# Grouping the attention products of a graph layer and moving its residual additions within the block

## The chip, the cores and the metric

The kernel runs on one core of a Trainium2 chip. The metric is the time of one execution on the device in microseconds; lower is better. A core has a matrix engine (TensorE, PE in the profile, with its weight loads as PEld), a vector engine (VectorE, DVE), an activation engine (ScalarE, ACT), a general engine (GpSimd, POOL) and an engine that here issues nearly all transfers (SyncE, SP). Each runs its own queue of instructions in the order of the program and waits on semaphores for the others.

## The reference

The input `x` holds 128 graphs of 64 nodes with 768 features, `adj` their 64 x 64 adjacency matrices. The features are normalised and rectified, go through two layers of the same kind, and the result is added to `x`:

```
h = max(layernorm(x), 0)
for l in 0, 1:
    u = triangular mix of (h W_left h^T) and (h W_right h^T) / sqrt(768)
    e = exp(u) * adj
    attention = e / (sum(e, axis=2) + 1e-10)
    h_lin = h W_lin + b_lin
    ctx = attention @ h_lin
    h = max((ctx - mean) / (std + 0.001) * ln_a + ln_b, 0)
out = x + h
```

All of it is float32. What matters here is the end of the second layer: `ctx`, its normalisation, the rectifier and the addition of `x` (the residual).

## The kernel before, in words

The 128 graphs are cut into NB = 16 blocks of 8 graphs, 512 nodes each. Each layer has two passes over the blocks. `pass_one` makes the attention matrices and leaves them in DRAM. `pass_two`, which the change touches, makes `h_lin` with a fast scheme of 15 block products in place of 18, multiplies by the attention, and normalises. `last` is true in layer two.

In `pass_two`, `linear(u, ...)` runs the 15 products of block `u` in the order of the list `ORDER`. Products share four accumulators named X, Z, Y and V in `ORDER`; the profile shows the tiles' own names, through `NAME`: X is tile Z there, Z is V, Y is X, V is Y. Accumulator X serves products 0, 2, 4, 6, 8 and 10, Y serves 3, 7 and 11, V serves 5, 9, 12 and 14, Z serves 1 and 13. A product adds to what its accumulator holds, and `read` (L300 for ScalarE, the helper at L245 for VectorE) moves the running sum into `hl` after each; the next product of the same accumulator has to wait for that read. The matrix products have line L1006. `fresh` (L995) starts an accumulator, by a ScalarE copy of the bias where one is wanted. The mean of `h_lin` is taken out of the weights beforehand, so that only the standard deviation is left to work out.

The order is written by hand (`manual_schedule`): each block has 30 slots, two a product, one run in the middle of the product and one after its reads, and `put(n, f)` hangs a piece of work on slot n; a slot of 30 or more is carried to the next block. All engines' instructions are issued in that one order, so a slot says behind what a piece of work stands on its engine's queue, not when it runs. SP issues a transfer when it comes to it and all that it must wait for is done, and may be far ahead of the others.

At the head of block u, ahead of slot 0, `load_h` (L368) asks for the tokens of block u+1: two tiles `ht` of 768 KB. ScalarE scales and rectifies them at slots 9 to 14 (`affine`, L379, two activations a slot, one on each of the two tiles), and POOL makes sums of them from slot 15 on (L245). `load_at` (L1036) brings the attention at slot 4.

The attention products of block u-1 and what follows them run inside block u. Two functions can do this. `finish(u, r)` makes half a block: `context` multiplies 16 small products into both buffers of the PSUM tile `aux` (L1048), ScalarE squares and sums them (L1193) and takes the root (L1195), VectorE inverts it (L1198, L1199). In layer two VectorE then scales by that and by `ln_a` (L1203), POOL adds `ln_b` (L1206), and `done` lets VectorE rectify and add the residual tile `xr` (L1217); two stores a tile go out from SP (L1219). `residual` (L1133) loads the two `xr` tiles of half a block with four transfers. `finish_block(u, more)` makes the whole block with one group of products (L1071), which writes to `aux` and to accumulators X and Y; VectorE copies the two parts that lie there away (L1143), the squares follow at slots 25 to 29 (L1154), the deviation and its inverse at 30 and 32 (L1158 to L1163), the scaling at 33 to 36 (L1168). A block has four row tiles, named (r, k) by half and place.

Before the change layer one uses `finish_block` for blocks 0 to 12 and `finish` for the last ones. Layer two uses `finish` throughout: the first half after product 0 of the next block with its steps at slots 6, 7, 8, 11, 12, the second half after product 7 with its steps at 20, 21, 22, 30, 30. The loads of the next residual half hang on the second `done` of each half. The last block of layer two has a form of its own (`last_block`, `finish_last`).

Of the kernel before, what the change touches and what calls it, by code (L numbers as in the profile page):

```python
# [10 lines left out]
F32 = mybir.dt.float32  # L11
I32 = mybir.dt.int32
AF = mybir.ActivationFunctionType
ALU = mybir.AluOpType
# [3 lines left out]
def kernel(  # L18
# [12 lines left out]
    nc = tc.nc  # L31
    B, S, H = x.shape
    L = w_lin.shape[0]
    P = 128
# [4 lines left out]
    PAIR = P // S  # L39
# [3 lines left out]
    NB = B * S // T  # L43
# [12 lines left out]
    NBB = T // S  # L56
# [10 lines left out]
    def put(slot, *fs):  # L67
        plan.setdefault(slot, []).extend(fs)
# [880 lines left out]
    rows = {}  # L949
# [62 lines left out]
    def pass_two(l, aside):  # L1012
        last = l == L - 1
        with tc.tile_pool(name=f"two{l}", bufs=2, reuse_waits="tile") as sp, \
# [59 lines left out]
            def batch(r, k, h):  # L1074
                return 4 * (h if k == 0 else 1 - h) + r + 2 * k

            XS = {}
# [27 lines left out]
            def finish_last(u, r):  # L1105


                cx = context(u, r)
                zs = [sp.tile([P, H], F32, name="z", bufs=4) for _ in range(2)]
                squares = sp.tile([P, Q, H], F32, name="hl", bufs=2)  # L1110
                two = "p (n d) -> p n d"
                xs = XS[u, r]
                of = stat.tile([P, 2, 2], F32, name="of", bufs=1)
                ss, rs = ([of[:, n, k:k + 1] for k in range(2)] for n in range(2))
                for k in (1, 0):
                    nc.scalar.activation(squares[:, k].rearrange(two, n=2), cx[k], AF.Square, accum_out=ss[k])
                    nc.vector.tensor_tensor(zs[1 - k].rearrange(two, n=2), cx[1 - k],  # L1117
                                            rows["a"].rearrange(two, n=2), op=ALU.mult)
                    nc.scalar.activation(rs[k], ss[k], AF.Sqrt, bias=floor, scale=1.0 / (H - 1.0))
                for k in (1, 0):  # L1120
                    nc.vector.tensor_scalar_add(rs[k], rs[k], EPS_LN)  # L1121
                    nc.vector.reciprocal(rs[k], rs[k])  # L1122
                    nc.vector.scalar_tensor_tensor(zs[k], zs[k], rs[k], rows["-b"], op0=ALU.mult, op1=ALU.max)  # L1123
                    nc.vector.tensor_add(xs[k], xs[k], zs[k])  # L1124
                    for h, queue in enumerate((nc.sync, nc.scalar)):
                        queue.dma_start(out[u * NBB + batch(r, k, h)], xs[k][h * S:(h + 1) * S])
                return []

            def residual(u, r):
                XS[u, r] = [sp.tile([P, H], F32, name="xr", bufs=4) for _ in range(2)]  # L1130
                for k in range(2):
                    for h in range(PAIR):
                        nc.sync.dma_start(XS[u, r][k][h * S:(h + 1) * S], x[u * NBB + batch(r, k, h)])  # L1133

            def finish_block(u, more):

                parts = context_block(u)
                tiles = ((0, 0), (0, 1), (1, 0), (1, 1))
                zs = {t: sp.tile([P, H], F32, name="z", bufs=4) for t in tiles}
                cut = (slice(0, T), slice(T, H))  # L1140

                for t in ((1, 1), (1, 0)):
                    nc.vector.tensor_copy(zs[t][:, cut[0]], parts[t][0])  # L1143
                    parts[t][0] = zs[t][:, cut[0]]
                    if t == (1, 1):
                        AHEAD.append(fresh(l, 0, more))
                ss = stat.tile([P, Q, 2], F32, name="ssb", bufs=2)
                sd = stat.tile([P, Q], F32, name="sdb", bufs=2)
                rs = stat.tile([P, Q], F32, name="rsb", bufs=2)

                def squares(t):
                    junk = zs[0, t[1]]
                    for n in range(2):
                        nc.scalar.activation(junk[:, cut[n]], parts[t][n], AF.Square,  # L1154
                                             accum_out=ss[:, 2 * t[0] + t[1], n:n + 1])

                def deviation():
                    nc.vector.reduce_sum(sd, ss, axis=mybir.AxisListType.X)  # L1158
                    nc.scalar.activation(sd, sd, AF.Sqrt, bias=floor, scale=1.0 / (H - 1.0))

                def inverse():
                    nc.vector.tensor_scalar_add(rs, sd, EPS_LN)
                    nc.vector.reciprocal(rs, rs)  # L1163

                def scaled(t):
                    by = rs[:, 2 * t[0] + t[1]:2 * t[0] + t[1] + 1]
                    for n in range(2):
                        nc.scalar.activation(zs[t][:, cut[n]], parts[t][n], AF.Copy, scale=by)  # L1168
                    kept(u, *t, zs[t])

                order = ((1, 1), (1, 0), (0, 0), (0, 1))
                for f, slots in ((squares, (25, 26, 28, 29)), (scaled, (33, 34, 35, 36))):
                    for n, t in zip(slots, order):
                        put(n, lambda f=f, t=t: f(t))
                put(30, deviation)
                put(32, inverse)

            def kept(u, r, k, z):
                for h in range(PAIR):
                    nc.sync.dma_start(ROWS[u][batch(r, k, h)], z[h * S:(h + 1) * S])  # L1180

            def finish(u, r):

                cx = context(u, r)
                zs = [sp.tile([P, H], F32, name="z", bufs=4) for _ in range(2)]
                if last and not u and not r:
                    residual(u, r)
                two = "p (n d) -> p n d"
                ss = stat.tile([P, 2], F32, name="ss", bufs=2)
                sd = stat.tile([P, 2], F32, name="sd1", bufs=2)  # L1190
                rs = stat.tile([P, 2], F32, name="rs1", bufs=2)
                for k in range(2):
                    nc.scalar.activation(zs[k].rearrange(two, n=2), cx[k], AF.Square, accum_out=ss[:, k:k + 1])  # L1193

                nc.scalar.activation(sd, ss, AF.Sqrt, bias=floor, scale=1.0 / (H - 1.0))  # L1195

                def inverse():
                    nc.vector.tensor_scalar_add(rs, sd, EPS_LN)  # L1198
                    nc.vector.reciprocal(rs, rs)  # L1199

                def scaled(k):
                    if last:
                        nc.vector.scalar_tensor_tensor(  # L1203
                            zs[k].rearrange(two, n=2), cx[k], rs[:, k:k + 1],
                            rows["a"].rearrange(two, n=2), op0=ALU.mult, op1=ALU.mult)
                        nc.gpsimd.tensor_add(zs[k], zs[k], rows["b"])  # L1206
                        return
                    if (u, r, k) == (NB - 1, 1, 1):
                        nc.vector.tensor_scalar_mul(zs[k].rearrange(two, n=2), cx[k], rs[:, k:k + 1])
                    else:  # L1210
                        nc.scalar.activation(zs[k].rearrange(two, n=2), cx[k], AF.Copy, scale=rs[:, k:k + 1])
                    kept(u, r, k, zs[k])

                def done(k):
                    if last:
                        xs = XS[u, r]
                        nc.vector.scalar_tensor_tensor(xs[k], zs[k], 0.0, xs[k], op0=ALU.max, op1=ALU.add)  # L1217
                        for h in range(PAIR):
                            nc.sync.dma_start(out[u * NBB + batch(r, k, h)], xs[k][h * S:(h + 1) * S])  # L1219
                        if k and u + r < NB - 1 and (u, r) != (NB - 2, 0):  # L1220
                            residual(u + r, 1 - r)

                steps = [lambda f=f, k=k: f(k) for f in (scaled, done) for k in range(2)]
                return [inverse] + (steps if last else steps[:2])

# [35 lines left out]
            for u in range(NB):  # L1261
                turn = not last and u >= NB - 2
                put(4, lambda u=u: load_at(u))
                if u + 1 < NB:
# [11 lines left out]
                        aside[u]()  # L1276
                    ends = {}
                    if u and last:
                        ends = {0: ((u - 1, 0), (6, 7, 8, 11, 12)), 7: ((u - 1, 1), (20, 21, 22, 30, 30))}
                    elif u > NB - 3:  # L1280
                        ends = {5: ((u - 1, 0), (16, 17, 18)), 11: ((u - 1, 1), (28, 29, 30))}
                    elif u:
                        ends = {12: (u - 1, None)}
# [3 lines left out]
                else:  # L1287
# [8 lines left out]
                                {4: ((u, 0), (50, 51, 52))})  # L1296
                    else:
                        last_block(u)
                        put(8, lambda: residual(u - 1, 1))
                        ends = ({0: ((u - 1, 0), (12, 13, 15, 19, 31)), 9: ((u - 1, 1), (28, 29, 30, 39, 41))},  # L1300
                                {2: ((u, 0), (44, 48, 51, 61, 62))})
                    linear(u, (0,), 0, ends[0], (1,))
# [62 lines left out]
```

## Time and profile before

| what | value |
|---|---|
| median of 3 runs | 2648.96 us |
| lowest, highest | 2647.83, 2654.08 us |
| the profiled execution's own time | 2648.42 us |
| its span from the first to the last instruction | 2646.6 us |
| mean granted TensorE clock | 0.995 |

Layer two's second pass takes roughly the last sixth of the span, from about 2190 us on. A time in the views below counts from the span's start. A row of the timeline gives start and length in us, engine, line, operation, and the tile written, an arrow, and the tiles read; several like instructions in a row are merged into one with a count. A row of the waits names who waited, an arrow, for whom, then the total in us, how often, and the longest. A row of the groups by line gives the durations in ns as min/median/max.

### The profile page before, as it was taken

Reading aid. Unit: us, or ns where it says so; the run is one execution under the profiler, and the core shown is the slowest. Engines: PE = TensorE matmul, PEld = TensorE weight load, DVE = VectorE, ACT = ScalarE, POOL = GpSimd, SP = SyncE. Lnnn points to the kernel's source line nnn. Section 1 sums busy time; section 2 is a strip of 40 time slices with the busy share of each in tenths; the row PEclk is TensorE's granted clock in tenths of the full one; section 3 lists DMA queues with packets and bytes.
Section 4 is the critical chain, followed back from the end, with each engine's and each line's share of the span. In section 5 each row is a group of like instructions: output and inputs, shape, how many; then the busy total and the mean of one; then the engine's idle time right before and its main releaser. Section 6 shows DMA issues by size and latency. Waiting matters only on the chain. (4 is left out here: it accounts for less than half of the span.)

```text
span 2646.6 us, 47202 instructions
## 1 busy us (share of the span) xinstructions
PE 2591.6 (98%) x18122; PEld 2217.1 (84%) x18122; DVE 1780.6 (67%) x2888; ACT 935.4 (35%) x1969; POOL 1763.1 (67%) x1392
## 2 busy tenths in 40 slices
PE   9899999999999999999999999999999989999998
PEld 8788888888888888888798888888888878887886
DVE  7878787777768445554456667677666676666667
ACT  5522223223113244454542222122222335555453
POOL 4766676666668657676276666667666657878786
PEclk9999999999999999999999999999999999999999
DMA  7443534343421354445794424253532215555655
GB/s 220 113 111 86 124 93 110 93 119 79 98 60 56 123 156 149 159 139 182 219 282 101 121 68 108 71 129 93 136 98 70 67 49 157 157 167 166 177 161 146
DMA packets 258465, 331.84 MB, mean 125 GB/s; under 512 B 56002, under 2 KB 190402, under 8 KB 258242
## 3 DMA queue, kind: packets, MB, share of 16 engines
q1 hardware_dynamic: 241442, 320.56, 44.3%
q10 hardware_dynamic: 16800, 8.26, 1.2%
q8 instruction: 145, 2.38, 0.4%
q14 instruction: 78, 0.64, 0.1%
HBM read 213.39 MB, written 115.34 MB: 124 GB/s over the span
## 5 line engine op out<-in xcount | busy, mean ns | idle before, releaser
L245 POOL TENSOR_TENSOR g<-ht 128x512 f32<-128x512 f32 (+1 forms) x620 | 785.9, 1279 | 420.8 <-PE Z L702 71.6
L245 POOL TENSOR_TENSOR g<-g,g 128x512 f32<-128x512 f32 (+1 forms) x310 | 397.9, 1291 | 136.7 <-PE C L702 22.0
L245 POOL TENSOR_TENSOR g<-ht,g 128x512 f32<-128x512 f32 (+1 forms) x272 | 346.1, 1282 | 164.8 <-PE Z L702 42.8
L702 PE MATMUL X<-g,g 128*128 128x256 f32 (+1 forms) x1080 | 252.9, 377 | 6.0 <-DVE m L914 6.0
L1006 PE MATMUL Z<-g,g 128*128 128x256 f32 x1024 | 244.1, 380 | 3.5 <-ACT hl L300 3.2
L702 PE MATMUL C<-g,g 128*128 128x256 f32 x1008 | 239.7, 381 | 4.9 <-POOL g L245 2.2
L702 PEld LDWEIGHTS X<-g,g 128*128 128x128 f32 x1080 | 203.0, 191 | 34.8 <-DVE m L914 6.8
L702 PE MATMUL Y<-g,g 128*128 128x256 f32 (+1 forms) x968 | 225.7, 376 | 3.8 <-POOL g L245 3.8
L1006 PEld LDWEIGHTS Z<-g,g 128*128 128x128 f32 x1024 | 191.6, 190 | 35.8 <-issue 4.1
L379 ACT ACTIVATE ht<-ht,b_col,a_col 128x256 f32<-128x256 f32 x384 | 196.1, 591 | 69.0 <-DMA ht<-h 53.8
L702 PEld LDWEIGHTS C<-g,g 128*128 128x128 f32 x1008 | 190.5, 190 | 32.9 <-POOL g L245 3.5
L702 PE MATMUL Z<-g,g 128*128 128x256 f32 (+1 forms) x936 | 217.0, 375 | 0.0
L702 PE MATMUL D<-g,g 128*128 128x256 f32 x880 | 209.8, 381 | 1.8 <-POOL g L245 1.8
L702 PEld LDWEIGHTS Y<-g,g 128*128 128x128 f32 x968 | 182.0, 190 | 27.8 <-POOL g L245 4.2
L702 PE MATMUL V<-g,g 128*128 128x256 f32 (+1 forms) x840 | 194.6, 375 | 3.1 <-POOL g L245 1.6
L702 PEld LDWEIGHTS Z<-g,g 128*128 128x128 f32 x936 | 174.5, 190 | 23.1
L702 PEld LDWEIGHTS D<-g,g 128*128 128x128 f32 x880 | 168.1, 191 | 25.7 <-POOL g L245 2.5
L1006 PE MATMUL X<-g,g 128*128 128x256 f32 x768 | 182.7, 379 | 0.0
L702 PEld LDWEIGHTS V<-g,g 128*128 128x128 f32 x840 | 157.6, 191 | 23.3 <-POOL g L245 1.7
L1206 POOL TENSOR_TENSOR z<-z,b 128x768 f32<-128x768 f32 x62 | 112.7, 1829 | 81.7 <-DVE z L1203 77.2
L245 DVE TENSOR_TENSOR m<-m,Y 128x512 f32<-128x512 f32 (+2 forms) x196 | 126.5, 667 | 58.4 <-ACT m L910 35.7
L245 DVE TENSOR_TENSOR m<-m,D 128x512 f32<-128x512 f32 x180 | 118.2, 677 | 70.0 <-ACT m L910 51.3
(222 smaller groups left out, 4612.0 us busy)
## 6 DMA issues: line engine op xcount, KB each, us to landing
ht<-h SPq DMA_DIRECT2D x126, 768.0 KB, 6.3
h<-xb SPq DMA_DIRECT2D x124, 384.0 KB, 6.6
z<-z SPq DMA_DIRECT2D x128, 192.0 KB, 3.1
x<-z SPq DMA_DIRECT2D x128, 192.0 KB, 5.4
xr<-in_x_dram SPq DMA_DIRECT2D x120, 192.0 KB, 3.8
out_dram<-xr SPq DMA_DIRECT2D x120, 192.0 KB, 2.7
x<-in_x_dram SPq DMA_DIRECT2D x112, 192.0 KB, 5.4
g<-form SPq DMA_DIRECT2D x40, 256.0 KB, 5.6
```

The lines of the kernel that those rows point to most:

```text
L245: (eng.tensor_add if sign == "+" else eng.tensor_sub)(o, a, b)
L379: nc.scalar.activation(ht, ht, AF.Relu, bias=cols[1][:, c:c + 1], scale=cols[0][:, c:c + 1])
L702: nc.tensor.matmul(o, w[:, c, g * P:(g + 1) * P], t, start=(new and g == c == at == 0), stop=(c == K2 - 1), skip_group_check=True)
L1006: nc.tensor.matmul(p[:, n], b[t][:, c, r * P:(r + 1) * P], w[s][:, c, :], start=(i in FIRST and i not in PRELOAD and n == c == 0), stop=(c ...
L1206: nc.gpsimd.tensor_add(zs[k], zs[k], rows["b"])
```

## The change

In layer two the attention products of blocks 0 to 12 are made by `finish_block`, as in layer one, called after product 12 of the next block. Blocks 13 and 14 keep `finish`, block 13 with its two halves after products 5 and 10 of block 14. In `finish_block` the scaling goes to VectorE with `ln_a`, in two parts a tile, POOL adds `ln_b`, and the new `done` adds the residual: tiles (0,0) and (0,1) at slots 39 and 42, which are slots 9 and 12 of the block after, tiles (1,0) and (1,1) at 58 and 61, which are slot 28 of that block and slot 1 of the one behind it. The residual loads no longer hang on `done`; they have slots of their own, 20 and 29 (13 and 29 in block 14, 3 and 9 in block 15). The tiles `z` get six buffers in place of four, the tiles `xr` five in place of four.

```diff
             def residual(u, r):
-                XS[u, r] = [sp.tile([P, H], F32, name="xr", bufs=4) for _ in range(2)]
+                XS[u, r] = [sp.tile([P, H], F32, name="xr", bufs=5) for _ in range(2)]
...
             def finish_block(u, more):
-                zs = {t: sp.tile([P, H], F32, name="z", bufs=4) for t in tiles}
+                zs = {t: sp.tile([P, H], F32, name="z", bufs=6 if last else 4) for t in tiles}
...
+                def done(t):
+                    z, xs = zs[t], XS[u, t[0]][t[1]]
+                    nc.vector.scalar_tensor_tensor(xs, z, 0.0, xs, op0=ALU.max, op1=ALU.add)
+                    for h in range(PAIR):
+                        nc.sync.dma_start(out[u * NBB + batch(*t, h)], xs[h * S:(h + 1) * S])
+
                 def scaled(t):
                     by = rs[:, 2 * t[0] + t[1]:2 * t[0] + t[1] + 1]
                     for n in range(2):
-                        nc.scalar.activation(zs[t][:, cut[n]], parts[t][n], AF.Copy, scale=by)
-                    kept(u, *t, zs[t])
+                        if last:
+                            nc.vector.scalar_tensor_tensor(zs[t][:, cut[n]], parts[t][n], by, rows["a"][:, cut[n]],
+                                                           op0=ALU.mult, op1=ALU.mult)
+                        else:
+                            nc.scalar.activation(zs[t][:, cut[n]], parts[t][n], AF.Copy, scale=by)
+                    if last:
+                        nc.gpsimd.tensor_add(zs[t], zs[t], rows["b"])
+                    else:
+                        kept(u, *t, zs[t])
 
                 order = ((1, 1), (1, 0), (0, 0), (0, 1))
-                for f, slots in ((squares, (25, 26, 28, 29)), (scaled, (33, 34, 35, 36))):
+                if last:
+                    order = ((0, 0), (0, 1), (1, 0), (1, 1))
+                for f, slots in ((squares, (25, 26, 28, 29)), (scaled, (33, 34, 35, 36))) + (
+                        ((done, (39, 42, 58, 61)),) if last else ()):
...
             def finish(u, r):
-                if last and not u and not r:
-                    residual(u, r)
...
-                        if k and u + r < NB - 1 and (u, r) != (NB - 2, 0):
-                            residual(u + r, 1 - r)
...
                     if u and last:
-                        ends = {0: ((u - 1, 0), (6, 7, 8, 11, 12)), 7: ((u - 1, 1), (20, 21, 22, 30, 30))}
+                        for r in range(2):
+                            put(29 if r else 20 if u < NB - 2 else 13, lambda u=u, r=r: residual(u - 1, r))
+                    if u > NB - 3 and last:
+                        ends = {5: ((u - 1, 0), (16, 17, 18, 21, 22)), 10: ((u - 1, 1), (25, 26, 27, 36, 38))}
                     elif u > NB - 3:
                         ends = {5: ((u - 1, 0), (16, 17, 18)), 11: ((u - 1, 1), (28, 29, 30))}
...
                         last_block(u)
-                        put(8, lambda: residual(u - 1, 1))
+                        put(3, lambda: residual(u - 1, 0))
+                        put(9, lambda: residual(u - 1, 1))
```

The tiles `z` of `finish` and `finish_last` get six buffers too.

More of the change, by code (lines that the diff above doesn't have):

```diff
@@ L1108, in finish_last @@
                 cx = context(u, r)
-                zs = [sp.tile([P, H], F32, name="z", bufs=4) for _ in range(2)]
+                zs = [sp.tile([P, H], F32, name="z", bufs=6) for _ in range(2)]
                 squares = sp.tile([P, Q, H], F32, name="hl", bufs=2)
@@ L1184, in finish @@
                 cx = context(u, r)
-                zs = [sp.tile([P, H], F32, name="z", bufs=4) for _ in range(2)]
-                if last and not u and not r:
-                    residual(u, r)
+                zs = [sp.tile([P, H], F32, name="z", bufs=6 if last else 4) for _ in range(2)]
                 two = "p (n d) -> p n d"
```

## The prediction

> **What bounds the kernel now.** I read the page's busy table first, then who waits for whom in the stretch that the change touches (layer two's second pass, 2190 to 2600 us), then the cost of one block there beside a block of layer one's second pass, which already has the form that the change brings.
>
> ```profile
> span 2646.6 us, 47202 instructions
> ...
> PE 2591.6 (98%) x18122; PEld 2217.1 (84%) x18122; DVE 1780.6 (67%) x2888; ACT 935.4 (35%) x1969; POOL 1763.1 (67%) x1392
> ```
>
> ```profile
> engine line waited for: us in total, times, longest us
> ACT hl L300 <- PE Z L1006: 141.4, 41, 6.7
> ...
> POOL g L245 <- ACT ht L379: 6.6, 14, 0.5
> ```
>
> In this stretch every engine waits for TensorE or for one another; no row has PE itself waiting. So the stretch ends with TensorE, and the change can win only what it takes from TensorE's queue, and loses whatever makes TensorE wait. The price of a block is the distance between equal places in neighbouring blocks (windows: length, then busy time of PE, PEld, DVE, ACT, POOL):
>
> ```profile
> 1088.95:1117.79 28.84, 28.84 (x157) 23.76 (x159) 15.76 (x23) 13.34 (x35) 20.63 (x17) 1.00 0.29 88
> 2370.35:2399.55 29.20, 29.20 (x153) 23.59 (x153) 19.93 (x25) 15.08 (x32) 23.20 (x16) 1.00 0.57 167
> ```
>
> The first row is layer one (one group of attention products a block, L1071), the second layer two (two groups, L1048). TensorE is busy through both at full clock. The difference is 0.36 us.
>
> **The change, part by part.**
>
> *Products.* Blocks 1 to 13 of layer two go from two groups to one: 13 x 0.36 = **4.7 us less**. Block 14 keeps two, block 15 its own form. Nothing else leaves TensorE's queue.
>
> *Copies, squares, scaling.* One group adds two VectorE copies a block (0.69 and 0.68 us, as the layer-one rows below have them) and cuts four scalings into eight. VectorE has 19.93 of 29.20 us busy, so some 3 us more fit; the copies, the preload behind them and the squares stand where layer one has them, under TensorE at full cover. I cost this at nothing; without cover it is the third rival.
>
> *The residual additions and loads.* Here the order on SP's queue changes, and SP issues strictly in program order. These are its rows for one block now:
>
> ```profile
> 2371.02 3.05 SPq L1219 DMA_DIRECT2D out_dram<-xr  x4
> 2374.12 2.52 SPq L1133 DMA_DIRECT2D xr<-in_x_dram  x4
> 2376.74 1.00 SPq L1036 DMA_DIRECT2D at<-att  x2
> 2383.50 3.05 SPq L1219 DMA_DIRECT2D out_dram<-xr  x4
> 2386.59 2.52 SPq L1133 DMA_DIRECT2D xr<-in_x_dram  x4
> 2389.28 0.95 SPq L368 DMA_DIRECT2D ht<-h  x2
> ```
>
> The last row is the load of the token halves `ht` for the block after the next boundary. It stands at the head of the next block's code, but SP reaches it 10.3 us before that block's first context group (2399.55), since the last thing ahead of it is the addition at slot 12. After the change the last things ahead of it are the addition of tile (1,0) at slot 28 with two stores, and four residual loads at slot 29. SP stands still at the store until VectorE has added. That wait has the rest of SP's queue behind it: first the four residual loads, then the two `ht` loads.
>
> When does it come now? The block's last products and VectorE's reads of them, in layer one, where the order of the last three products is that of the new kernel:
>
> ```profile
> 1091.62 1.99 PE L1006 MATMUL V<-g,g 128*128 128x256 f32 x8
> 1093.45 1.89 PE L1006 MATMUL Y<-g,g 128*128 128x256 f32 x8
> 1095.18 1.03 PE L1006 MATMUL Z<-g,g 128*128 128x256 f32 x4
> ```
>
> ```profile
> 1090.04 0.69 DVE L1143 COPY z<-Z 128x512 f32<-128x512 f32 x1 [0.36 <-PE Z L1071]
> 1090.65 0.68 DVE L1143 COPY z<-X 128x512 f32<-128x512 f32 x1
> ...
> 1093.66 0.69 DVE L245 TENSOR_TENSOR hl<-hl,V 128x512 f32<-128x512 f32 x1 [1.73 <-PE V L1006]
> ```
>
> Let S be the start of the next block's first product, 1095.18. VectorE reads product 13 from S-1.52; the addition at slot 28 is next in its queue and begins 0.61 later, at S-0.91. Its length (min, median, max in ns), then the row of landing times of the 108 stores of L1219, then that of the 28 loads of the tile `ht`, both in this stretch:
>
> ```profile
> L1217 DVE SCALAR_TENSOR_TENSOR xr<-z,xr x60: 951/2023/2432, 2206.2 to 2626.0; 128x768 f32<-128x768 f32 x60
> ```
>
> ```profile
> DMA to landing us min/median/max: 2.6/2.7/4.1
> ```
>
> ```profile
> DMA to landing us min/median/max: 4.4/6.6/8.1
> ```
>
> With the median 2.02 us the addition ends at S+1.11. SP issues the two stores at S+1.14 and S+1.74 (0.6 each), the second lands 2.7 later at S+4.45. The first residual tile's two loads go out meanwhile. With five `xr` buffers the second tile takes the buffer of the very tile just stored (four tiles a block: tile (1,1) of one block is five after tile (1,0) of the block before), so SP waits until S+4.5; two issues of 0.64, and the `ht` loads go out at S+5.9 and S+6.53. The landing row gives 4.4 to 8.1 us. I take 6.4, a little under the median, because two loads instead of four stand right before. The second half then lands at **S+12.9**.
>
> When is it needed? Now ScalarE and TensorE in the middle of a block:
>
> ```profile
> 2378.82 1.89 PE L1006 MATMUL Y<-g,ht 128*128 128x256 f32 x8
> 2380.54 1.89 PE L1006 MATMUL Z<-g,g 128*128 128x256 f32 x8
> 2382.27 1.89 PE L1006 MATMUL X<-g,g 128*128 128x256 f32 x8
> 2384.09 1.52 PE L1048 MATMUL aux<-hl,at 64*64 64x384 f32 x16
> 2385.54 1.99 PE L1006 MATMUL Z<-g,ht 128*128 128x256 f32 x8
> ```
>
> ```profile
> 2379.02 0.60 ACT L300 ACTIVATE hl<-Z 128x512 f32<-128x512 f32 x1 [2.37 <-PE Z L1006]
> 2379.51 4.03 ACT L379 ACTIVATE ht<-ht,b_col,a_col 128x256 f32<-128x256 f32 x8
> 2383.44 0.58 ACT L300 ACTIVATE hl<-Z 128x512 f32<-128x512 f32 x1
> ```
>
> The PE rows are products 5, 6, 7, a context group, 8. ScalarE reads product 4, puts eight `ht` activations through (first and second half in turn), then reads product 6, out of the bank on which product 8 accumulates. That read ends at 2384.02, 5.20 us after product 5 began. Product 8 has until then 1.5 us in hand, which is the context group; the change moves that group to the block's end, and three products of 1.73 are 5.19: **no slack is left**. Any delay of the activations becomes a wait of TensorE before product 8. The second activation (first of the second half) begins 1.18 after product 5's start, that is at S + 5 x 1.73 + 1.18 = S+9.83. The half lands at S+12.9: **3.1 us of wait a block**.
>
> It first happens in block 3 (the first store at slot 28 is in block 2) and last in block 14, which still loads block 15: 12 blocks, 12 x 3.1 = 37.2 us. Bounds: with the shortest addition (0.95) and the quickest load (4.4) nothing is left (below nothing isn't possible, since TensorE's products stay); with 2.43 and 8.1 it is 5.2 us, 62 us in all.
>
> *The clock.* TensorE's granted clock after its two longest waits behind VectorE (2.9 and 3.1 us):
>
> ```profile
> PE X L702 <- DVE m L914: 6.0, 2, 3.1
> ```
>
> ```profile
> 834.00:838.00 4.00, 1.10 (x6) 0.70 (x5) 3.96 (x5) 0.83 (x2) 3.70 (x3) 1.00 0.00 0
> ...
> 2134.00:2136.00 2.00, 0.12 (x1) 0.00 (x0) 1.97 (x2) 0.42 (x1) 2.00 (x2) 1.00 0.00 0
> 2136.00:2138.00 2.00, 0.78 (x2) 0.69 (x3) 2.00 (x4) 0.42 (x1) 1.70 (x2) 0.66 0.00 0
> 2138.00:2140.00 2.00, 2.00 (x7) 1.55 (x6) 2.00 (x4) 0.00 (x0) 0.36 (x1) 0.50 0.00 0
> 2140.00:2142.00 2.00, 2.00 (x11) 1.77 (x10) 2.00 (x5) 0.00 (x0) 2.00 (x2) 0.98 0.00 0
> ```
>
> After the first the clock (third number from the right) stays at 1.00; after the second it is half for about 3.4 us (0.34 x 2 / 0.5 + 2 + 0.08), which costs 1.7 us of products. One of two: I estimate half of the twelve waits, 6 x 1.7 = 10 us; bounds 0 and 20.
>
> The Trainium skill ("TensorE: Matmul & The Clock Gate", Part 1) has the clock fall to half only after a whole idle window of about 3.4 us. By that rule a wait of 3.1 us would cost no clock and the sum would come out about 10 us lower; the 2136 row, a fall after 3.1 us, speaks against it here.
>
> *Sum*, against the profiled execution's 2648.42 us (span 2646.6 and 1.8 around it; the median shown is 2648.96, 0.5 above): 2648.4 - 4.7 + 37.2 + 10 = **2691**.
>
> **Rivals.**
>
> *A, on the other side: the load is early enough.* If SP got past slot 28 before the block ends, as it now does 10 us ahead, only the products would change: 2648.4 - 4.7 = 2644, not slower. It decides at one point: the second half must land before S+9.9. Against it: even with no wait on the buffer the stores and four issues put the second load at about S+4.9, and the quickest landing of 4.4 gives S+9.3; for it: that and a 0.95 us addition would do. It is within 0.3% of before, which is about what a measurement of this kernel can tell from no change; the 0.3% are 7.9 us. 0.15.
>
> *B: late loads, clock kept.* The waits come in but stay too short or too badly placed for the clock: 2648.4 - 4.7 + 37.2 = 2681. 0.25.
>
> *C: VectorE becomes the bound.* Scaling at slots 3 to 6 (some 5 us with 1.0 us a tile and more where POOL slows it) plus an addition of 2 us at slot 1 puts the read of product 3 close to product 7, which accumulates in that bank, at S+12.1. I reckon its end at S+10.4 to S+11.8. If it alone were 1 us late, 12 us come in: 2656. 0.05.
>
> *Forecast*: late loads with some clock loss, 2691. 0.55.
>
> **The numbers.** Slower by over 0.3% (above 2656.9) holds the forecast, B, and half of C: 0.82. Within: most of A, the rest of C: 0.16. Faster by over 0.3% (below 2641.0) needs more than the products can give: 0.02. The range leaves out A and the far end: at 2659 the wait is 1.3 us a block without clock loss (2648.4 - 4.7 + 15.6), at 2718 it is 4.5 us with the clock lost in every block (2648.4 - 4.7 + 54 + 20).
>
> **What would show it.** Right: TensorE waits for ScalarE's `hl` read at L300 about a dozen times, some 3 us each, between products 7 and 8; ScalarE waits at L379 for the DMA `ht<-h`; SP's `ht` issues stand 5 to 6 us behind the block's first product; blocks of about 32 to 34 us; granted clock under 1.00 in some. Wrong: blocks of 28.84 us with no PE wait (A); TensorE waiting for VectorE's `hl` reads (C); landings much quicker than 6 us once the residual loads are out of step; additions of 1 us where POOL is idle at slot 28.

## The result and the profile after

The changed kernel takes 2711.92 us (median of 4 runs, 2705.91 to 2716.52) where the kernel before takes 2648.48 on the same chip: a ratio of 1.0231, 95% interval 1.0218 to 1.0243, slower by 63 us. The profiled execution took 2711.45 us with a span of 2709.7, against 2648.42 and 2646.6 before.

The page's first lines, then who made TensorE wait, and for whom ScalarE waited, in blocks 3 to 14 of layer two's second pass (2253 to 2650 us):

```profile
span 2709.7 us, 47249 instructions
...
PE 2610.5 (96%) x18122; PEld 2235.2 (82%) x18122; DVE 1792.2 (66%) x2953; ACT 944.0 (35%) x2060; POOL 1753.0 (65%) x1392
```

```profile
engine line waited for: us in total, times, longest us
...
PE Z L1006 <- ACT hl L300: 38.2, 12, 4.8
ACT ht L379 <- DMA ht<-h: 37.1, 23, 2.9
```

Before, TensorE had no wait in this stretch. Now it has twelve, one a block, all for ScalarE's read into `hl`; and ScalarE's own new wait, almost as long in sum, is for the token load. The same in the windows of four blocks (length, then busy time of PE, PEld, DVE, ACT, POOL, then the granted clock): block 2, where the load is still in time, blocks 5 and 6, and block 12.

```profile
2224.11:2253.13 29.02, 29.02 (x154) 23.74 (x153) 19.96 (x28) 16.89 (x41) 22.76 (x15) 1.00 0.21 55
2322.36:2356.29 33.93, 30.79 (x153) 24.94 (x152) 20.74 (x30) 15.79 (x41) 22.39 (x15) 0.95 0.48 144
2356.29:2390.16 33.87, 30.80 (x154) 24.98 (x153) 20.76 (x30) 15.80 (x41) 22.38 (x15) 0.95 0.49 144
2560.82:2591.63 30.81, 29.10 (x153) 23.73 (x152) 20.75 (x30) 15.79 (x41) 23.06 (x15) 1.00 0.55 159
```

Block 2 is 29.02 us, 0.18 under the 29.20 of before. Block 6 is 4.85 longer than block 2: 3.07 of wait, and 1.78 more busy time for the same work, of which the clock at 0.95 explains 1.7. Block 12 waited 1.71 us and kept its clock. Now block 6 from its first product (2356.29) on, SP, VectorE and POOL:

```profile
2356.35 1.13 SPq L1169 DMA_DIRECT2D out_dram<-xr  x2
2357.58 3.12 SPq L1133 DMA_DIRECT2D xr<-in_x_dram  x4
2360.82 0.99 SPq L368 DMA_DIRECT2D ht<-h  x2
```

```profile
2354.77 0.69 DVE L245 TENSOR_TENSOR hl<-hl,V 128x512 f32<-128x512 f32 x1 [2.33 <-PE V L1006]
2355.37 0.95 DVE L1167 SCALAR_TENSOR_TENSOR xr<-z,xr 128x768 f32<-128x768 f32 x1
...
2370.00 1.97 DVE L1167 SCALAR_TENSOR_TENSOR xr<-z,xr 128x768 f32<-128x768 f32 x1
```

```profile
2349.80 2.52 POOL L245 TENSOR_TENSOR g<-ht 128x512 f32<-128x512 f32 x2
2362.40 8.76 POOL L1180 TENSOR_TENSOR z<-z,b 128x768 f32<-128x768 f32 x4 [10.07 <-DVE z L1175]
```

And what ScalarE and TensorE make of it:

```profile
2366.60 0.60 ACT L379 ACTIVATE ht<-ht,b_col,a_col 128x256 f32<-128x256 f32 x1 [0.88 <-DMA ht<-h]
2369.26 3.55 ACT L379 ACTIVATE ht<-ht,b_col,a_col 128x256 f32<-128x256 f32 x7 [2.06 <-DMA ht<-h]
2372.71 0.57 ACT L300 ACTIVATE hl<-Z 128x512 f32<-128x512 f32 x1
```

```profile
2368.38 1.89 PE L1006 MATMUL X<-g,g 128*128 128x256 f32 x8
2373.34 2.88 PE L1006 MATMUL Z<-g,ht 128*128 128x256 f32 x8 [3.07 <-ACT hl L300]
```

The addition at slot 28 runs at 2355.37, its stores go out at 2356.35, four residual loads follow, and the token loads stand at 2360.82, 4.5 us into the block (before, they went out 10 us ahead of the block's first context group). The first activation waits for the first half, the second for the second half until 2369.23, seven run through, the read of product 6 ends at 2373.28, and product 8 starts. It would have started 1.73 after product 7, at 2370.1. The row of product 8 is 2.88 us long instead of the 2.00 that it has in block 2: the clock was halved within it.

In the last two blocks TensorE waits at two places more, both times for VectorE, which has an addition of block 12 or 13 in front of the read, and two groups of attention products take 2.2 us instead of 1.52:

```profile
2635.96 2.19 PE L1048 MATMUL aux<-hl,at 64*64 64x384 f32 x16
...
2659.22 1.97 PE L1006 MATMUL Y<-g,g 128*128 128x256 f32 x8 [1.04 <-DVE hl L245]
...
2665.37 1.50 PE L1048 MATMUL aux<-hl,at 64*64 64x384 f32 x10 [1.42 <-DVE hl L245]
...
2674.94 2.18 PE L1048 MATMUL aux<-hl,at 64*64 64x384 f32 x16
```

In these two groups the trace puts the pause before a weight load (0.49 and 0.48 us) down to VectorE's scalings (L1175, L1217), which read the `aux` buffer that the group writes next.

Where the 63.1 us of the two spans went (the kernel after, block by block, against 29.20):

| part | us |
|---|---|
| blocks 1 to 13 shorter by 0.18 each | -2.3 |
| twelve waits before product 8, blocks 3 to 14 | +38.2 |
| clock halved after eleven of the twelve, 1.7 each | +18.7 |
| rest of block 14 (35.51, less 2.7 wait and 1.7 clock) | +1.9 |
| last block (48.64 against 44.53) | +4.1 |
| everything ahead of the pass (it starts at 2157.81 against 2155.98) | +1.8 |
| sum | 62.4 |

The 1.8 us ahead of the pass are no effect of the change: in the traces of the experiments, whose code up to there is the same, the pass starts anywhere from 2157.75 to 2164.53.

### The profile page after: what moved, and what is told of

It reads as the page before. It is cut to its first block, busy times and chain, and to the rows that moved or that the text cites. A ratio compares the mean times of both kernels' runs of the same rounds, so it can differ in the third digit from the quotient of the medians.

```text
span 2709.7 us, 47249 instructions
## 1 busy us (share of the span) xinstructions
PE 2610.5 (96%) x18122; PEld 2235.2 (82%) x18122; DVE 1792.2 (66%) x2953; ACT 944.0 (35%) x2060; POOL 1753.0 (65%) x1392
## 5 line engine op out<-in xcount | busy, mean ns | idle before, releaser
L245 POOL TENSOR_TENSOR g<-ht 128x512 f32<-128x512 f32 (+1 forms) x620 | 764.5, 1245 | 445.7 <-ACT ht L379 105.4
L245 POOL TENSOR_TENSOR g<-ht,g 128x512 f32<-128x512 f32 (+1 forms) x272 | 335.5, 1242 | 162.7 <-PE Z L702 43.2
L1006 PEld LDWEIGHTS Z<-g,g 128*128 128x128 f32 x1024 | 192.5, 190 | 35.6 <-issue 3.5
L245 DVE TENSOR_TENSOR hl<-hl,Z 128x512 f32<-128x512 f32 (+1 forms) x136 | 83.2, 652 | 157.6 <-PE Z L1006 143.1
L1006 PE MATMUL Z<-g,ht 128*128 128x256 f32 x512 | 136.4, 413 | 42.2 <-ACT hl L300 42.2
```

The costliest lines, as they stand in the source:

```text
L245: (eng.tensor_add if sign == "+" else eng.tensor_sub)(o, a, b)
L1006: nc.tensor.matmul(p[:, n], b[t][:, c, r * P:(r + 1) * P], w[s][:, c, :], start=(i in FIRST and i not in PRELOAD and n == c == 0), stop=(c ...
```

## The experiments

The theory to test: the token load stands too late in SP's queue, ScalarE's activations wait for it, and its read of product 6, which stands behind them, holds up product 8. The rivals: ScalarE has lost its slack whenever the load comes; the additions at the block's end crowd VectorE; the clock's fall is only a record and costs nothing. All ratios are to the kernel before on the same chip; its median there was 2652.0 to 2653.8 us.

**The load ahead.** The changed kernel with the load moved:

```diff
-                    load_h(2, l, u + 1, u == 0)
+                    if not (last and u > 1):
+                        load_h(2, l, u + 1, u == 0)
+                    if last and u and u + 2 < NB:
+                        put(14, lambda u=u: load_h(2, l, u + 2))
```

> The changed kernel, but the token load for the block after next is issued at slot 14 of each block, ahead of the residual loads and the late stores. My theory (the load stands too late in SyncE's queue, so ScalarE's activations and with them its read before product 8 come late): the twelve waits of 38 us and the falls of the clock go, blocks of about 29.0 us, 2655 to 2658 us in all. Rival (ScalarE has no slack left once the attention group has moved, whenever the load comes): waits of 1 us or more a block stay, 2670 us or more. Rival (the additions at the block's end crowd VectorE): nothing changes, about 2711 us.

2657.35 us, ratio 1.0018 (1.0008 to 1.0027). The queue of SP in one block, and a block's window:

```profile
2297.67 3.61 SPq L1169 DMA_DIRECT2D out_dram<-xr  x4
2301.38 1.02 SPq L368 DMA_DIRECT2D ht<-h  x2
2302.46 3.32 SPq L1133 DMA_DIRECT2D xr<-in_x_dram  x4
```

```profile
2284.46:2313.48 29.02, 29.02 (x154) 23.69 (x153) 21.79 (x30) 15.55 (x41) 23.09 (x16) 1.00 0.59 168
```

The load goes out 17 us into the block before its use. All of blocks 1 to 13 are 29.02 us, the waits and the clock's falls in them are gone, with every late addition where it was. The theory holds. The late additions as such cost these blocks nothing, and of the rival that ScalarE has no slack whenever the load comes, 0.18 us a block are left. The last two blocks are still longer than before: 31.78 and 48.60 us against 29.20 and 44.53.

**Only the order of two loads.** The slot-29 residual loads behind the token load:

```diff
-                            put(29 if r else 20 if u < NB - 2 else 13, lambda u=u, r=r: residual(u - 1, r))
+                            put(30 if r else 20 if u < NB - 2 else 13, lambda u=u, r=r: residual(u - 1, r))
```

> The changed kernel, but the four residual loads of slot 29 stand one slot later, behind the token load; the addition at slot 28 and its stores still stand ahead of it. My theory: the token load goes out about 3.3 us earlier, its second half lands about 9.7 us into the block, just when it is needed; waits of 0 to 0.5 us a block, 2655 to 2663 us. Rival (the wait for the addition and its stores is what makes the load late, not the loads ahead of it): waits of about 2 us stay, 2685 us or more.

2672.13 us, ratio 1.0067 (1.0052 to 1.0082). TensorE's waits in the pass:

```profile
PE Z L1006 <- ACT hl L300: 10.5, 11, 1.9
```

Most of the loss is gone (waits of 10.5 instead of 38.2, no fall of the clock in blocks 3 to 14), so the four loads ahead of the token load were the larger part; but not all, and more stayed than I expected. The load does go out 3.2 us earlier, at 1.3 to 2.5 us into the block; its second half lands at 10.0 to 11.7, not at 9.7. The rows of one pair of token loads, issue to landing, in the kernel before, in the changed one, and here:

```profile
DMA to landing us min/median/max: 5.6/6.2/6.8
```

```profile
DMA to landing us min/median/max: 5.8/6.8/7.8
```

```profile
DMA to landing us min/median/max: 5.5/7.5/9.4
```

The minimum is the first half, the maximum the second, issued 0.6 later. The halves land 1.8, 2.6 and 4.5 us apart: with nothing issued behind them for 10 us, with stores behind them, with four loads behind them. Over all pairs of these blocks it is 1.8 without exception in the kernel before, 1.8 to 3.0 in the changed one, and 3.1 to 4.5 here; the load of the first experiment, with four loads behind it too, has 2.9 to 3.1. This suggests that what is issued later slows what is still on its way; no run tests it by itself.

**Half a dose.** Only the second residual tile of slot 29, the one that waits for its buffer, goes behind the token load; `residual` gets the places that it loads as a third argument:

```diff
-                            put(29 if r else 20 if u < NB - 2 else 13, lambda u=u, r=r: residual(u - 1, r))
+                            put(29 if r else 20 if u < NB - 2 else 13, lambda u=u, r=r: residual(u - 1, r, (0,) if r else (0, 1)))
+                        put(30, lambda u=u: residual(u - 1, 1, (1,)))
```

> A half dose: only the second residual tile of slot 29, the one that waits for a buffer, stands behind the token load. My theory: the load goes out about 1.9 us earlier, waits of about 1.2 us a block (12 x 1.2 = 14 us), too short for the clock to fall often, about 2669 us, between the kernel with both tiles behind the load and the changed kernel. Rival (a threshold, not a sum: the load is either in time or a whole queue late): either like the changed kernel, 2711 us, or with no wait, 2656 us.

2697.28 us, ratio 1.0154 (1.0128 to 1.0181), waits:

```profile
PE Z L1006 <- ACT hl L300: 29.2, 12, 3.2
```

Between the two others, so it is a sum and no threshold, but 28 us above my number. The load goes out 1.9 us earlier, at 2.6; the second half lands at 12.0 to 13.1, only some 0.7 earlier; two loads now stand behind it, which fits the reading above. The waits are 2.4 us on average, long enough to halve the clock in five of the twelve blocks.

**The load late, ScalarE's queue another.** Nothing at SP; the activations at slots 15 to 20 and the sums from 21 on:

```diff
-                    put_all(9 if u else 15, affine(2, l, u + 1))
-                    put_sums_t((2, l, u + 1), 15 if u else 21, 1, 0)
+                    put_all(15 if last or not u else 9, affine(2, l, u + 1))
+                    put_sums_t((2, l, u + 1), 21 if last or not u else 15, 1, 0)
```

> The changed kernel with its late token load as it is, but ScalarE's activations of the tokens stand at slots 15 to 20 instead of 9 to 14, and POOL's sums from slot 21 on. My theory (the late load hurts only because ScalarE's read of product 6 stands behind the activations in its queue): no wait before product 8, 2655 to 2662 us, a little more if POOL's sums come late. Rival (the late load hurts TensorE by another way, through the sums or the memory traffic): waits stay or move to POOL's sums, 2680 us or more.

2656.81 us, ratio 1.0013 (1.0003 to 1.0023), TensorE with no wait in blocks 1 to 14, and blocks 1 to 13 as in layer one:

```profile
2298.84:2327.68 28.84, 28.84 (x154) 23.77 (x153) 22.68 (x30) 15.81 (x40) 23.86 (x16) 1.00 0.59 169
```

In these blocks the late load hurts only through what stands behind the activations in ScalarE's queue. The block is 28.84 us, not 29.02: also with the load in time 0.18 us was lost before product 8. Part of what is won goes into the last block, 54.5 us against 48.6 in the changed kernel.

**The late load alone, in the kernel before.** Two attention groups as ever; only the load moves, from the head of a block to slot 1:

```diff
-                    load_h(2, l, u + 1, u == 0)
+                    if last and u > 1:
+                        put(1, lambda u=u: load_h(2, l, u + 1))
+                    else:
+                        load_h(2, l, u + 1, u == 0)
```

> The kernel before, with only the token load moved from the head of a block to slot 1, behind the two late additions' stores and four residual loads; the two attention groups a block stay. My theory: the load goes out about 8 us into the block, its second half lands 14.5 to 16.5 us in, needed at 11.5, and the attention group after product 7 gives 1.5 us of slack: waits of 2 to 3.5 us in 13 blocks, with part of the clock lost 2685 to 2715 us. Rival (late loads hurt only in the new grouping): 2649 to 2655 us.

2711.52 us, ratio 1.0236 (1.0216 to 1.0255): a loss as large as the change's, without the change.

```profile
2370.17 2.53 SPq L1133 DMA_DIRECT2D xr<-in_x_dram  x4
2372.86 0.96 SPq L368 DMA_DIRECT2D ht<-h  x2
```

```profile
2378.32 1.89 PE L1006 MATMUL X<-g,g 128*128 128x256 f32 x8
2380.14 1.52 PE L1048 MATMUL aux<-hl,at 64*64 64x384 f32 x16
2384.46 1.99 PE L1006 MATMUL Z<-g,ht 128*128 128x256 f32 x8 [2.79 <-ACT hl L300]
```

The load goes out 8.3 us into the block; the context group between products 7 and 8 hides 1.5 us, and 2.8 stay. Thirteen waits, 42 us in all. That the two losses are equal is chance, since the load goes out 3.8 us later here than in the changed kernel and the context group hides part of that. But a late load alone is enough for such a loss, and the grouping with the load ahead costs only 0.2% (1.0018).

**The price of the clock.** The changed kernel with products of no use between products 7 and 8 (`for n in range(12)` first, then 6), written to `aux` and read by nothing:

```diff
+                    if last and i == 7 and 2 < u < NB - 2:
+                        fill = ps_aux.tile([P, 2, T], F32, name="aux")
+                        b, w = tokens_of((2, l, u))["B4"], W[l, "n"][8]
+                        for n in range(12):
+                            nc.tensor.matmul(fill[:, 0, :D], b[:, n % 2, :P], w[:, n % 2, :], start=True, stop=True)
```

> The changed kernel with twelve extra products of no use (2.6 us, their result is read by nothing) between products 7 and 8 of blocks 3 to 13, so that TensorE works where it waited. If the fall of the clock after the waits costs what its rows say (1.7 us in ten of these blocks), the clock stays at full speed and the time falls by 15 to 17 us to about 2695 us. If the fall costs nothing or comes from something else than the wait, the time stays at 2711 us or rises to 2715.

2714.84 us, ratio 1.0241 (1.0225 to 1.0257).

```profile
2287.77:2321.79 34.02, 34.02 (x178) 28.33 (x177) 20.77 (x30) 15.80 (x41) 23.07 (x15) 1.00 0.49 144
```

I had the dose wrong: the twelve took 5.0 us (34.02 - 29.02), more than the wait. The run tells only that a TensorE that works through keeps its clock. With six:

> The changed kernel with six extra products between products 7 and 8 of blocks 3 to 13. Twelve took 5.0 us a block, not 2.6 (each is two passes), longer than the wait, so the blocks were 34.02 us each and told only that the clock stays up; six take 2.5 to 2.6 us, a little less than the mean wait of 3.2 us. If the fall of the clock costs what its rows say: blocks of 31.6 to 33 us, no fall of the clock in them, about 2694 us, 15 to 18 us under the changed kernel though TensorE does more work. If it costs nothing: about 2711 us.

2699.61 us, ratio 1.0173 (1.0158 to 1.0187), 15 us below the changed kernel by the two ratios (0.0058 x 2650).

```profile
2289.40:2321.64 32.24, 31.69 (x166) 25.97 (x165) 20.74 (x30) 15.79 (x41) 22.39 (x15) 1.00 0.52 151
2321.64:2353.69 32.05, 31.70 (x166) 25.98 (x165) 20.75 (x30) 15.79 (x41) 22.40 (x15) 1.00 0.53 153
```

Two windows of a block's length, blocks 4 and 5: 32.1 us at full clock where the changed kernel has 33.8, though TensorE does 2.6 us more. Blocks 3 to 13 are 32.50 on average against 33.85. The clock fell in two blocks in place of eleven, one of them not filled. Of the 4.83 us by which the changed kernel's blocks exceed 29.02, ten falls in eleven blocks make 1.55 and leave 3.28; here the excess is 3.48, one fall makes 0.15 and leaves 3.33. The delay before product 8 is thus the same in both, and the difference is the clock. So the fall is real time, and it comes from TensorE's idling.

**A better version?** Load ahead, as in the first experiment, and the activations from slot 7 on:

```diff
-                    put_all(9 if u else 15, affine(2, l, u + 1))
+                    put_all((7 if last and u > 1 else 9) if u else 15, affine(2, l, u + 1))
```

> The changed kernel with the token load at slot 14 of the block before and ScalarE's activations from slot 7 on instead of 9. My theory: the slack before product 8, which moved away with the attention group, is there again, so the 0.18 us a block that TensorE still loses with loads in time go too: blocks of 28.84 us, some 2 us less than with the early load alone, 2653 to 2655 us. Rival (the 0.18 us come from something else): the same as with the early load alone.

2658.29 us, ratio 1.0022 (1.0013 to 1.0032); blocks again of 29.02. My step was wrong: at slots 7 to 12 all twelve activations stand ahead of the read of product 6, instead of eight, and what is won in front is lost behind.

Then the last two additions of block 12 earlier, with the activations still at 7 to 12:

```diff
-                        ((done, (39, 42, 58, 61)),) if last else ()):
+                        ((done, (39, 42, 46, 49) if u == NB - 4 else (39, 42, 58, 61)),) if last else ()):
```

> As the kernel with load and activations ahead, and the last two additions of block 12 stand at slots 46 and 49 instead of 58 and 61, out of the way of the halves of block 13. My theory: the changed kernel's last two blocks are some 6 us longer than before because VectorE has these additions in front of its reads there; they go for the most part, 2647 to 2650 us, level with the kernel before or up to 2 us faster. Rival (the last blocks are longer for the residual loads, which come late on SyncE): no gain over the kernel with load and activations ahead.

2655.02 us, ratio 1.0014 (1.0005 to 1.0023). Block 14 is 32.62 instead of 31.78, the last 46.73 instead of 48.72: a gain of 1.1 us in the trace, not the 6 expected, and the two ratios' intervals overlap.

On top of it, the activations at slots 7, 8, 9, 10, 13, 14:

```diff
-                    put_all((7 if last and u > 1 else 9) if u else 15, affine(2, l, u + 1))
+                    at = (7, 8, 9, 10, 13, 14) if last and u > 1 else range(9 if u else 15, 15 if u else 21)
+                    for n, f in zip(at, affine(2, l, u + 1)):
+                        put(n, f)
```

> As the kernel with load and activations ahead and the last additions of block 12 moved, but the activations at slots 7, 8, 9, 10, 13 and 14. At 7 to 12 all twelve stood ahead of ScalarE's read of product 6, so the two slots won at the start were lost at the end and the blocks stayed at 29.02 us; now eight stand ahead, from slot 7 on. My theory (the 0.18 us a block are the missing slack before product 8): 28.84 us a block, 13 x 0.18 = 2.3 us less than with the last additions moved alone, about 0.1% under it. Rival (they come from something else in the grouping): 29.02 us again.

2653.70 us, ratio 0.9999 (0.9990 to 1.0008).

```profile
2288.48:2317.32 28.84, 28.84 (x154) 23.78 (x153) 21.00 (x30) 15.83 (x41) 23.79 (x16) 1.00 0.58 169
```

Now blocks 2 to 13 have the layer-one length. The missing slack was the 0.18 us.

On top of that, the first two additions of block 13 later:

```diff
-                        ends = {5: ((u - 1, 0), (16, 17, 18, 21, 22)), 10: ((u - 1, 1), (25, 26, 27, 36, 38))}
+                        ends = {5: ((u - 1, 0), (16, 17, 18, 28, 31)), 10: ((u - 1, 1), (25, 26, 27, 36, 38))}
```

> As the kernel with split activations, and the two additions of block 13's first half at slots 28 and 31 of block 14 instead of 21 and 22, where VectorE stood 1.7 us for POOL's sum with its reads behind it. My theory (the last blocks are longer because additions stand ahead of VectorE's reads): block 14 falls from 32.6 towards 30 us, the whole to the kernel before or 1 to 3 us under it. Rival (block 14 is longer for the place of its two attention groups after products 5 and 10): no change in block 14.

2653.20 us, ratio 1.0001 (0.9992 to 1.0010); block 14 is 30.64 instead of 32.63, the last block 48.79 instead of 46.73. The expectation came true for block 14 alone; the time only moved into the last block. And still later:

```diff
-                        ends = {5: ((u - 1, 0), (16, 17, 18, 28, 31)), 10: ((u - 1, 1), (25, 26, 27, 36, 38))}
+                        ends = {5: ((u - 1, 0), (16, 17, 18, 31, 33)), 10: ((u - 1, 1), (25, 26, 27, 36, 38))}
-                        put(3, lambda: residual(u - 1, 0))
+                        put(4, lambda: residual(u - 1, 0))
```

> As the kernel with the tail's first half moved, but block 13's first two additions stand at slots 31 and 33, behind the attention group that opens the last block, and the residual load of block 14's first half at slot 4 of it. That group waited 1.4 us for VectorE's read of product 14, which stood behind one of these additions. My theory (each addition ahead of a read that TensorE waits for costs about its own length): the 1.4 us go, the whole 1 to 3 us under the kernel before. Rival (the last block is longer for the additions wherever they stand, since they all fall into it now): block 14 gets shorter and the last block longer by the same, level with the kernel before.

2654.86 us, ratio 1.0002 (0.9992 to 1.0011), block 14 at 30.63, the last at 48.84. The wait ahead of the context group is gone, and another has come later in the block, behind a ScalarE preload:

```profile
2613.48 1.10 PE L1006 MATMUL X<-g,g 128*128 128x256 f32 x4 [0.31 <-DVE hl L245]
2614.41 1.03 PE L1006 MATMUL Z<-g,ht 128*128 128x256 f32 x4
2617.06 1.13 PE L1006 MATMUL Y<-g,ht 128*128 128x256 f32 x4 [1.62 <-ACT Y L995]
```

The rival is borne out: at all the places tried since the additions of block 12 were moved (four versions), the last two blocks are together 5.6 to 5.7 us longer than before, and that eats the 4.5 us that the grouping wins. No version here beats the kernel before; three are level with it. Whether the last two blocks could be ordered so that the 4.5 us stay was not settled.

## Why the prediction was right, point by point

The forecast was 2691 us in a range of 2659 to 2718, by late loads; it came out at 2712 by late loads. The mechanism, the twelve blocks, the place of the wait and its size were as forecast, the size in part by luck. The 20 us between the two are the clock (8.7 more), the tail (6.0), the products (2.4 less won), the part ahead of the pass (1.8) and the waits (1.0).

- *Products, 4.7 us less.* Too good: 2.3. The prediction found that no slack was left before product 8 and yet set its own cost at nothing. Also with the load in time (block 2) product 8 starts 1.81 us after product 7 instead of 1.73, and product 9 another 1.83 behind it, which makes the 0.18; the split activations give it back (28.84).
- *When the load goes out, 5.9 us into the block.* It was 4.5. The step that failed is the length of the addition at slot 28, taken from the median of 2.02 us; POOL is idle there (2352.3 to 2362.4, from its two rows), and the addition took 0.95; of the 60 rows behind the median all but one have POOL at work beside them. The one at slot 12, beside POOL, took 1.97. That is 1.1 of the 1.4 us. SP did wait for the stored buffer, as said (14 waits, 8.5 us in all).
- *Landing of the second half, 6.4 us.* It was 7.8 in block 6 (5.1 to 12.9 us into the block). I went by the row's 6.6, which mixes first and second halves; the second halves alone took 6.8 to 8.1 us already in the kernel before, 7.5 on average over the six recorded, against 7.6 over the twelve in the changed kernel. So the stores that now stand behind the load are not needed to explain it. The two errors cancel, which is luck: 12.9 forecast, 12.9 in block 6, 11.6 to 14.7 over the twelve.
- *When it is needed, and the wait.* 3.1 us in twelve blocks, 37.2 in all; measured 38.2 in the same twelve blocks, before product 8, behind the same read.
- *The clock, 10 us.* Half of the waits was an estimate from one row in two; it fell in eleven of twelve, 18.7 us. This is the term that was furthest off; the last section shows what decides a fall. By the rule of the Trainium skill ("TensorE: Matmul & The Clock Gate", Part 1), a whole idle window of about 3.4 us, only four of the twelve waits would have been long enough; the measurement decides, and it says that waits of 2.3 to 3.4 us do it too.
- *The tail.* I set it at nothing, and block 14 and the last block cost 6 us besides. Their VectorE work had no cover: the additions pushed behind block 12 fall in front of reads that TensorE waits for. At those two places TensorE loses some 4.6 us against before (1.2 at product 14 of block 14, 3.4 within the group that opens the last block); the two slow attention groups are the other 1.3.
- Rival A would have been 2644. With the load ahead the ratio is 1.0018: its condition is met, its price was not: 2644, 2.3 for the 0.18 us a block and 6.7 for the tail make 2653, and 1.0018 of 2648.4 is 2653. Rival C, TensorE waiting for VectorE's reads, showed nothing in the full blocks; in the tail its wait is there.

## What to carry to other kernels

When work is moved later in a hand-written order, look first at what the queue that stores or loads for it carries behind it: here a prefetch that had run a third of a block ahead of its need was put behind a store that waits for a result of the block's end. In this kernel it was enough to issue the prefetch ahead of the block's late store and the loads behind it. And before a filler is taken out of the middle of a chain, ask which engine used it as slack; a wait of 3 us of a matrix engine that was busy for 98% of the time costs its length, and here in most blocks the clock on top.

## Not expected of the hardware

TensorE's clock halved after waits of 2.3 to 4.8 us and kept at 1.7 us in the changed kernel; between 2.1 and 2.9 us both were seen (with the second tile behind the load, a wait of 2.33 us halved it and one of 2.42 us did not; in the kernel before with the late load, one of 2.79 us did not). So there the length alone doesn't decide.

The traces show what does. Within a trace the falls in this pass lie whole multiples of 3.413 us apart; in the changed kernel they begin at 2271.897, 2306.030, 2340.163 and so on, ten steps each. Blocks 1 to 14 can be cut into steps of that grid. In all 14 traces together these blocks have 27 falls, each at the end of a step in which TensorE was idle for 0.61 of the time or more; no step with 0.56 or less has one at its end, and no step at full clock lies between. Here are the two waits of 2.42 and 2.33 us in steps (length, busy times, then the granted clock):

```profile
2398.08:2401.50 3.42, 2.34 (x11) 1.71 (x9) 3.42 (x4) 2.75 (x6) 3.22 (x2) 1.00 0.56 166
2401.50:2404.91 3.41, 2.07 (x10) 1.84 (x11) 0.62 (x1) 3.41 (x8) 2.94 (x3) 1.00 0.75 189
2404.91:2408.32 3.41, 3.41 (x17) 2.94 (x16) 1.97 (x3) 0.84 (x2) 3.33 (x3) 1.00 0.88 228
...
2462.94:2466.35 3.41, 1.08 (x6) 0.90 (x6) 1.78 (x1) 3.41 (x8) 2.91 (x3) 1.00 0.60 147
2466.35:2469.76 3.41, 3.41 (x10) 2.67 (x9) 1.29 (x2) 1.92 (x4) 3.25 (x4) 0.50 0.98 268
```

The longer wait is split over two steps (1.08 and 1.34 idle of 3.41), and the clock stays; the shorter one lies in one step (2.33 idle), and the next step runs at half clock. The two rows on which the prediction's one in two rests come out alike, 0.54 for the wait that kept the clock and 0.74 for the one that lost it. It also suggests why so many waits of the changed kernel lost it: a block with wait and fall is 33.1 to 35.6 us long, near ten steps (34.13), so that one wait after the other meets the grid at about the same place. This is read off the traces; no run moved a wait along the grid on purpose, and some falls in the last block and in other passes, after steps idle for as little as 0.38, don't fit.

A load seems to be slowed by what is issued after it on the same queue: the two halves of the token load land 1.8, 1.8 to 3.0 and 2.9 to 4.5 us apart with nothing, stores, and four loads behind them. From issue to landing the second half takes 6.8 to 8.1, 6.5 to 8.7 and 7.7 to 9.4 us in the same order, ranges that overlap. It was read off these rows and not measured by itself. The Trainium skill ("DMA: Bandwidth & Descriptors", Queues, rings and completion order) has the descriptors of a queue consumed in ring order on each engine, but a later one possibly finishing its write first. Whether that has to do with what these rows show, no run here tells.
